# Four adjacency layers: another way to the bias of layer 0, denominators tile by tile, and a new order around the last tile

## The chip, the cores and the metric

The kernel runs on one core of one Trainium2 chip. The metric is device microseconds (us) of one execution. Engines: PE (TensorE, matmuls; PEld is its weight load), DVE (VectorE), ACT (ScalarE), POOL (GpSimd), SP (SyncE, which only issues DMAs here). ACT and POOL issue DMAs as well. Each engine works through its own instructions in order.

## The reference, cut to what matters

Four layers work on x of shape 8 x 2048 x 64 (batch B = 8, nodes N = 2048, channels C = 64) with one adjacency matrix; each is `x = layernorm(x + layer(x))`. The change lies in layer 0 and in what layer 0 prepares for layer 1:

```python
# layer 0: K = 3 terms x, A x, 2 A(A x) - x; weights and bias per node by an embedding of 16 numbers
w = einsum('nd,dkio->nkio', embedding, weight)
b = einsum('nd,do->no', embedding, bias)            # 2048 x 64
out = einsum('bnki,nkio->bno', x_g, w) + b
# layer 1, the part that layer 0's tiles prepare
h = x @ W
s = leaky_relu(h @ a_node, 0.2)
alpha = softmax(where(H.T > 0, s, NEG))             # 64 hyperedges over 2048 nodes
agg = einsum('ben,bnf->bef', alpha, h)
```

`agg` is a sum over nodes of exp(s) h for the members of each hyperedge, divided by a denominator, the sum of exp(s) over the same members.

## The kernel before, in words

Nodes go in 16 tiles of 128 (NT = 16), and a tile row holds all 8 batches, 512 columns (BC). Products with the mask of the adjacency matrix split their dense operand in a high and a low part, so each takes two matmuls. The stretch that matters has four parts.

**First product** (`first_product`, from L453): y1 = A x. Its 32 pieces of the matrix are numbered n = 0 to 31; `begin(n)` loads piece n (`raw`), makes the mask `m` from it on DVE (L519) and, for the first eight, loads x (`xraw`) and splits it on ACT (x_hi, L471) and DVE (x_lo, L472). `begin` runs two pieces ahead of the matmuls (L560), of which a piece has 16. PSUM buffers come in turn from one pool of seven (`ps_acc`): `warm`, four `y1p` per quarter, and two `bp`. Before the loop 16 warm-up matmuls run. At n = 1 `node_bias` (L476) makes the bias of all nodes: 16 matmuls of 16 rows by 64 columns from the transposed embedding `et`, loaded at the very start on ACT's queue (L1656). At n = 2 ACT copies them (`keep_bias`, L491) to `bn_all`. From n = 10 `midway` loads the weights of layer 0 and, last, the embedding `emb_sb` on SP's queue (L244). `steps` builds lists for layer 1 in between.

**Tiles of layer 0** (`layer0`, from L1075): the order is written out by hand in the loop from L1543, and `program_order` keeps PE, DVE, ACT and POOL to it. (SP's order is settled by the framework.) Each tile j has eight `weigh(j, g)`: 24 matmuls into one of two `pp` buffers (L1221), then four multiply-adds on DVE that read it (L1232). After each of them other steps are put: `normed(j - 1, 0..2)` normalises the tile before in three steps (sum, centring and square; variance and square root on ACT; reciprocal and scaling, and the store of x1 on SP's queue, L1259). After g = 4 comes `visit(j)`, the excursion: it gathers the weighted features of tile j - 2 into `aggp` (L1414), makes the second product of tile j + 1 (32 matmuls, L1184), masks for j + 2 on DVE (L449), comparisons of the matrix with its scaled mask on DVE (L1136), the transposes of x1 (`to_features`, L1309) and of y2 (`second_term`, L1194), and the degrees (L1203): one matmul with the mask's sum over POOL's `both` (L1131). After g = 5 and 7 `project` (L1364) multiplies with layer 1's weights (`hp`, L1336) and copies the results out (`hi` and `h` and `sc` on ACT, `lo` on DVE); `weights_of` (L1369) makes exp(s) in `es`, `weighted` (L1394) the weighted features on POOL. Transposes, degrees and `hp` share the two PSUM buffers `tr`.

**Last tile** (`last_tile`, L1497): tile 15 is normalised and projected in two halves of the batch (`half_normed`, `half_features`, `projected`, `copied`, `half_weighted`, `half_gather`). Before it `spread` (L1418) makes the membership masks `mds` of all 16 tiles anew, and `denominators` (L1429) multiplies them with `es`: 16 small fp32 matmuls, of two passes each, 15 of them in one run. `industry_early` (L1435) holds 16 steps of two matmuls of a product of layer 1 that needs nothing else; `early[0](n)` runs n of them wherever PE would wait.

**Start of layer 1** (`layer1`, from L584): `agg = aggp * rden` on DVE (L620), its exponential, transposes and two small products on PE (`fche` L645, `sep` L659, `dnp` L672), with `early` steps in between (L634, L641, L656); then the `ramp` (L1001), a hand-written order of the first units of work, in which `0.ind` runs what is left of `early`.

The order in the loop around g, which the change edits:

```python
                    elif g == 5:
                        ...
                        when(j - 1, project, 0)
                        if j == NT - 1:
                            half_normed(0, 0)
                            project(j - 1, 1)
                            weights_of(j - 1)
                    elif g == 6:
                        if j == NT - 1:
                            half_normed(0, 1)
                            weighted(j - 1)
```

## Time and profile before

| What | Value |
|---|---|
| Three runs | 1297.23, 1299.42, 1298.87 us; median 1298.87 |
| The profiled execution | 1296.06 us, its span 1294.3 us |
| PE busy, mean granted clock | 1228.0 us, 0.972 |
| First product | from 7.07 to 143.4 us (L560) |
| Weighing of layer 0's tiles | first L1221 at 157.13, last DVE step L1232 at 682.0 us |
| A whole tile in the middle | 32.66 us (from 628.26 to 660.92, the same matmul of two tiles) |
| `denp`, 32 matmul records L1431 | 7.0 us |
| `bp`, 32 matmul records L484 | 4.5 us |
| `agg` of layer 1, L620 | starts at 699.99 us |

How to read it: the profile is of one execution, and its times count from the start of the span. An fp32 matmul makes two records. "Idle before" is how long an engine did nothing before an instruction, with the instruction that released it. The granted clock is the share of full speed at which PE was allowed to run; a matmul at half clock counts as busy for twice as long. Pieces of the timeline name engine, line, operation, output and inputs.

### The profile page before, as it was taken

What the parts mean: (1) busy time and instruction counts of PE and PEld (TensorE: products, weight loads), DVE (VectorE), ACT (ScalarE), POOL (GpSimd) and SP (SyncE); (2) the same over time, 40 slices, a digit from 0 to 9 for tenths busy, and PEclk for the clock granted to TensorE, in tenths of its full rate; (3) what the DMA queues carried; (4) which work ended last, traced back from release to release, by engine and by line L of the source; (5) the groups of instructions that cost most, each with busy time, mean ns of one, the idle gap of its engine ahead of it and who ended that gap; (6) DMA issues with size and microseconds to landing.
All of it is one profiled execution on the core that took longest, in us unless ns stands there. A gap on an engine that the chain in (4) does not pass through costs nothing.

```text
span 1294.3 us, 19958 instructions
## 1 busy us (share of the span) xinstructions
PE 1228.0 (95%) x7598; PEld 1000.4 (77%) x7598; DVE 881.9 (68%) x1657; ACT 389.0 (30%) x987; POOL 503.4 (39%) x420
## 2 busy tenths in 40 slices
PE   9999989999999999999998799999998899999996
PEld 7877768888888888888886477777766788888885
DVE  5455378888787877777774777777774656565544
ACT  3000101222222222222232356666665521111111
POOL 1000282555555555555311678888871600000000
PEclk8999999999999999999997699999998999999998
DMA  8788742333333333332443222223220223324541
GB/s 293 195 237 207 187 122 89 103 108 104 105 107 102 105 106 106 105 108 96 168 134 98 89 91 101 99 92 105 83 69 1 98 99 129 128 101 155 192 173 68
DMA packets 100890, 157.23 MB, mean 121 GB/s; under 512 B 12785, under 2 KB 64113, under 8 KB 94897
## 3 DMA queue, kind: packets, MB, share of 16 engines
q1 hardware_dynamic: 98144, 151.51, 36.6%
q10 hardware_dynamic: 2464, 4.33, 0.9%
q8 instruction: 62, 1.02, 0.3%
q0 software_dynamic: 176, 0.02, 0.1%
q14 instruction: 44, 0.35, 0.1%
HBM read 118.08 MB, written 37.76 MB: 120 GB/s over the span
## 4 chain that ended last, share of the span: by engine, by line
PE 76%; DVE 9%; issue 7%; ACT 2%; DMA 2%; POOL 2%; SPq 0%; DVEq 0%; ACTq 0%; POOLq 0%
PE a L1671 18%; PE pp L1221 18%; PE ind L1671 9%; PE y2p L1184 9%; PE y1p L560 5%; DVE r L1232 5%; PE fc L914 3%; PE df L923 2%; PE gp L795 1%; PE yp L1771 1%; PE try L168 1%; PE trm L168 1%; PE hp L1336 1%; PE red L844 1%; DVE r L1241 1%
## 5 line engine op out<-in xcount | busy, mean ns | idle before, releaser
L1232 DVE SCALAR_TENSOR_TENSOR r<-pp,emb_sb,r 128x256 f32<-128x256 f32 x512 | 247.6, 484 | 87.9 <-PE pp L1221 72.5
L1221 PE MATMUL pp<-w_sb,xT 64*128 64x256 f32 x1024 | 160.3, 385 | 11.3 <-DVE r L1232 9.6
L1221 PE MATMUL pp<-w_sb,y2T 64*128 64x256 f32 x1024 | 156.7, 377 | 0.0
L1221 PE MATMUL pp<-w_sb,y1T 64*128 64x256 f32 x1024 | 156.7, 377 | 0.0
L1120 POOL TENSOR_TENSOR ms<-msk,srow 128x1024 f32<-128x1024 f32 x32 | 87.0, 2720 | 103.0 <-DVE msk L449 93.3
L1221 PEld LDWEIGHTS pp<-w_sb,xT 64*128 64x128 f32 x1024 | 97.8, 188 | 25.2 <-PE pp L1221 15.6
L1221 PEld LDWEIGHTS pp<-w_sb,y1T 64*128 64x128 f32 x1024 | 104.1, 188 | 8.2
L1221 PEld LDWEIGHTS pp<-w_sb,y2T 64*128 64x128 f32 x1024 | 103.9, 188 | 8.3
L560 PE MATMUL y1p<-x_hi,m 128*128 128x512 f32 x256 | 104.5, 408 | 0.7 <-ACT x_hi L471 0.7
L1184 PE MATMUL y2p<-y_hi,msk 128*128 128x512 f32 x256 | 102.5, 400 | 0.0
L560 PE MATMUL y1p<-x_lo,m 128*128 128x512 f32 x256 | 102.2, 399 | 0.2 <-DVE x_lo L472 0.2
L1671 PE MATMUL ind<-y_hi,mj_l 128*128 128x512 f32 x240 | 101.8, 424 | 0.2 <-DVE dlt L879 0.2
L1184 PE MATMUL y2p<-y_lo,msk 128*128 128x512 f32 x256 | 101.3, 396 | 0.0
L1671 PE MATMUL a<-v_hi,mj_l 128*128 128x512 f32 x256 | 100.1, 392 | 0.0
L1671 PE MATMUL a<-v_lo,mj_l 128*128 128x512 f32 x256 | 100.0, 391 | 0.0
L1671 PE MATMUL a<-y_lo,mj_l 128*128 128x512 f32 x240 | 95.1, 396 | 0.0
L1671 PE MATMUL a<-y_hi,mj_l 128*128 128x512 f32 x240 | 94.9, 395 | 0.0
L1671 PE MATMUL ind<-y_lo,mj_l 128*128 128x512 f32 x240 | 94.5, 394 | 0.0
L830 POOL TENSOR_TENSOR ez<-ez,coef 128x1024 f32<-128x1024 f32 x32 | 69.8, 2183 | 48.6 <-DVE ez L825 48.6
L1136 DVE SCALAR_TENSOR_TENSOR ms<-ms,adj 128x1024 f32<-128x1024 f32 x32 | 71.0, 2224 | 0.0
L1403 POOL TENSOR_TENSOR hs<-h,es 128x512 f32<-128x512 f32 x15 | 15.6, 1042 | 129.2 <-ACT hgr L1375 129.2
L560 PEld LDWEIGHTS y1p<-x_hi,m 128*128 128x128 f32 x256 | 49.1, 192 | 12.2 <-ACT x_hi L471 0.9
(298 smaller groups left out, 2410.5 us busy)
## 6 DMA issues: line engine op xcount, KB each, us to landing
mj_l<-mask SPq DMA_DIRECT2D x46, 1024.0 KB, 4.9
adj<-in_at SPq DMA_DIRECT2D x64, 256.0 KB, 3.9
mask<-msk SPq DMA_DIRECT2D x32, 512.0 KB, 4.0
raw<-in_at SPq DMA_DIRECT2D x31, 512.0 KB, 5.4
oh<-oh SPq DMA_DIRECT2D x32, 128.0 KB, 3.6
xT<-in_xt SPq DMA_DIRECT2D x16, 256.0 KB, 3.1
xs<-in_xn SPq DMA_DIRECT2D x16, 256.0 KB, 2.7
kept<-x SPq DMA_DIRECT2D x16, 256.0 KB, 2.0
```

The source lines that it names most:

```text
L168: nc.tensor.matmul(dst, src, ident, start=True, stop=True, is_transpose=True)
L560: nc.tensor.matmul(accs[q][jj], r_(m[:, t, jj * P:(jj + 1) * P]), r_(part[:, mt, :]), start=i + h + t == 0 and part is x_hi, stop=i == 3 a ...
L830: nc.gpsimd.tensor_tensor(by_b(ezs[i]), by_b(ezs[i]), per_b(t["coef"], 2 * i, 2), ALU.mult)
L914: nc.tensor.matmul(fc[:, h, :], fcw_sb[rs], sT[rs], start=True, stop=True)
L923: nc.tensor.matmul(df[:, b:b + 1], th[:, b % 2, (b // 2) * P:(b // 2 + 1) * P], av_sb, start=True, stop=True,)
L1120: nc.gpsimd.tensor_tensor(ms, m, srow[j].unsqueeze(1).to_broadcast([P, 8, P]), ALU.mult)
L1136: nc.vector.scalar_tensor_tensor(ms, ms, 1.0, raws[j][h], op0=ALU.mult, op1=ALU.not_equal, accum_out=bad[:, 2 * j + h:2 * j + h + 1],)
L1184: nc.tensor.matmul(acc, r_(msk[j, mt // 8][:, mt % 8, :]), r_(part[:, mt, :]), start=mt == 0 and part is y_hi, stop=mt == NT - 1 and part ...
L1221: nc.tensor.matmul(pp[:, h, pl, :], terms[j][name][rs, 2 * bq + pl], w_sb[rs, k, dq * 4 * C:(dq + 1) * 4 * C], start=k == 0, stop=k == K - 1,)
L1232: nc.vector.scalar_tensor_tensor(rb, ppv[:, :, dd, :], emb_sb[:, j, d:d + 1], rb, op0=ALU.mult, op1=ALU.add)
L1403: nc.gpsimd.tensor_tensor(b_view(hs), b_view(h_sb[:, j, :]), bcast(es[:, j, :]), ALU.mult)
L1671: nc.tensor.matmul(acc, r_(a[:, mt, :]), r_(part[:, mt, :]), start=mt == 0 and part is hi, stop=mt == NT - 1 and part is lo,)
```

## The change: what it does

The bias of layer 0 no longer comes from 16 thin matmuls. The embedding of eight tiles at a time (128 nodes by 8 x 16 numbers) is transposed on PE and copied by ACT, and one matmul per half multiplies it with `et[2]`, a block-diagonal matrix of eight copies of the bias, built by a memset and eight small loads on POOL's queue. For that the embedding is loaded before the loop on ACT's queue, and the transposed embedding and the separate bias are not loaded. The steps stand at n = 3 and n = 5, the copy out at n = 6. The warm-up matmuls alternate between two PSUM tiles.

`degrees` becomes `counted(j, i)`, which stands before `to_features` in the visit and adds the denominators of tile i = j - 3 of its argument, that is tile j - 2 of the visit: one fp32 matmul into the same PSUM tile and a second ACT copy; DVE adds it to `rden`. Only tiles 14 and 15 remain for `last_tile`. `spread` makes the mask of tile 15 alone.

The steps of `normed` move: 0 from after g = 0 to after g = 1, 1 from after g = 2 to the visit, 2 behind the first comparison of the visit (tile 14's stay). In the first tile the degrees, the second comparison and `scaled(1, 1)` move to after g = 2. In the last tile `project(14, 1)`, its weights and `industry_early` move, and `last_tile` has another order, with 6 + 3 + 1 `early` steps (before: 2); layer 1's start has 3 + 1 + 1 (before: 4 + 1 + 2), and `0.ind` runs the rest. `projected(15, 1)` takes a `pp` buffer instead of two `tr` ones. The cores of the diff:

```diff
-                nc.sync.dma_start(emb_sb, emb.rearrange("(t p) d -> p t d", p=P))
+                nc.scalar.dma_start(emb_sb, emb.rearrange("(t p) d -> p t d", p=P))
...
+                if step == 0:
+                    tr = ps_acc.tile([P, 2, P], F32, tag="acc", name="tr_et")
+                    for half in range(2):
+                        transpose(
+                            tr[:, half, :],
+                            emb_sb[:, half * NT // 2:(half + 1) * NT // 2, :]
+                            .rearrange("p t d -> p (t d)"),
+                        )
+                    for half in range(2):
+                        nc.scalar.copy(et[half][:, 0:P], tr[:, half, :])
+                    return
                 for half in range(2):
                     bp = ps_acc.tile([P, NT // 2, C], F32, tag="acc", name=f"bp_{half}")
...
+                    nc.tensor.matmul(
+                        bp.rearrange("p t c -> p (t c)"), et[half][:, 0:P], et[2],
+                        start=True, stop=True,
+                    )
...
+                for k in range(16):
+                    nc.tensor.matmul(warm[k % 2], ones, ones, start=True, stop=True)
                 begin(0)
                 begin(1)
+                midway(2 * K)
...
-                    if n == 1:
-                        node_bias()
-                    elif n == 2:
+                    if n in (3, 5):
+                        node_bias((n - 3) // 2)
+                    elif n == 6:
                         keep_bias()
...
-                early[0](4)
+                early[0](3)
...
-                early[0](2)
+                early[0](1)
...
+        def counted(j, i):
 
             dp = ps_tr.tile([P, QW], F32, tag="tr", name=f"dgp_{j}")
+            if j < NT:
+                nc.tensor.matmul(
+                    dp[:, 0:2], r_(msk[j, "sum"]), r_(ones_r), start=True, stop=True
+                )
+            if i >= 0:
+                nc.tensor.matmul(dp[:, 8:8 + B], mds[i], es[:, i, :], start=True, stop=True)
+                dens[i] = tile("den", f"den_{i}", (P, B), 1)
+                nc.scalar.copy(dens[i], dp[:, 8:8 + B])
+            if j < NT:
+                nc.scalar.copy(deg[:, j:j + 1], dp[:, 0:1])
...
             if j < NT - 1:
+                when(j - 1, normed, 1)
+            when(j + 1, compare, 0)
+            if j < NT - 1:
                 when(j - 1, normed, 2)
-            when(j + 1, compare, 0)
...
             when(j + 1, compare, 1)
+            counted(j + 1, j - 2)
             when(j - 1, to_features)
...
             when(j + 1, second_term)
-            when(j + 1, degrees)
+            if j == 2:
+                nc.vector.tensor_copy(rden, dens[j - 2])
+            elif j > 2:
+                nc.vector.tensor_tensor(rden, rden, dens[j - 2], ALU.add)
...
         def last_tile():
+            last = NT - 1
+            early[0](6)
             half_features(0)
+            gather(last - 1)
+            denp = ps_p.tile([P, 2, 2, 4 * C], F32, tag="pp", name="denp")[:, 0, 0, 0:B]
+            nc.tensor.matmul(denp, mds[last - 1], es[:, last - 1, :], start=True, stop=False)
+            projected(last, 0)
             half_normed(1, 0)
             half_normed(1, 1)
+            copied(last, 0, "sc")
+            weights_of(last, slice(0, 4))
+            copied(last, 0, "h")
+            copied(last, 0, "hi")
+            half_normed(1, 2)
             half_weighted(0)
+            copied(last, 0, "lo")
+            early[0](3)
+            half_features(1)
+            projected(last, 1)
+            copied(last, 1, "sc")
+            weights_of(last, slice(4, 8))
+            half_weighted(1)
+            early[0](1)
             half_gather(0)
+            nc.tensor.matmul(denp, mds[last], es[:, last, :], start=False, stop=True)
             half_gather(1)
+            nc.vector.tensor_tensor(rden, rden, denp, ALU.add)
...
+                        if j == NT - 1:
+                            normed(j - 1, 0)
                     elif g == 1:
+                        if j < NT - 1:
+                            when(j - 1, normed, 0)
+                        if j:
+                            when(j + 1, scaled, 1)
+                            when(j + 1, first_sum)
+                    elif g == 2 and j == NT - 1:
+                        normed(j - 1, 1)
+                    elif g == 2 and j == 0:
+                        compare(0, 1)
+                        counted(0, -1)
+                        scaled(1, 1)
...
                             half_normed(0, 0)
-                            project(j - 1, 1)
-                            weights_of(j - 1)
+                            early.extend(industry_early())
                     elif g == 6:
                         if j == NT - 1:
                             half_normed(0, 1)
+                            project(j - 1, 1)
+                            weights_of(j - 1)
                             weighted(j - 1)
...
+        et = [big.tile([P, BC], F32, tag=f"b1_{NT - 4 + q}", name=f"et_{q}") for q in range(3)]
+        nc.gpsimd.memset(et[2], 0.0)
+        for t in range(NT // 2):
+            nc.gpsimd.dma_start(et[2][t * D:(t + 1) * D, t * C:(t + 1) * C], bias0)
```

## The prediction, made before the changed kernel ran

> **What bounds the kernel now.** I read the page's shares first, then the PE clock in fine windows, then what PE waits for by stage, then the timelines at both ends of layer 0.
>
> ```profile
> PE 1228.0 (95%) x7598; PEld 1000.4 (77%) x7598; DVE 881.9 (68%) x1657; ACT 389.0 (30%) x987; POOL 503.4 (39%) x420
> PEclk8999999999999999999997699999998999999998
> ```
>
> PE is busy for 95% of the span and its clock is full except in three places of 32 us slices. So time can go only where PE idles, runs at half clock, or does work that is avoidable. The windows (columns: stretch, its length, busy time of PE, PEld, DVE, ACT, POOL, granted clock, DMA share, GB/s) show two such places:
>
> ```profile
> 11.00:15.00 4.00, 4.00 (x32) 3.64 (x31) 2.62 (x5) 1.22 (x3) 0.00 (x0) 0.92 1.00 359
> 15.00:19.00 4.00, 4.00 (x12) 3.21 (x12) 2.76 (x5) 1.14 (x2) 0.00 (x0) 0.50 0.93 315
> 19.00:23.00 4.00, 4.00 (x15) 3.18 (x14) 1.90 (x4) 2.11 (x4) 0.28 (x1) 0.73 0.88 332
> ...
> 680.00:684.00 4.00, 1.17 (x6) 0.49 (x3) 3.66 (x9) 0.79 (x2) 2.78 (x4) 0.92 0.20 66
> 684.00:688.00 4.00, 3.25 (x15) 2.30 (x15) 0.92 (x4) 1.34 (x8) 2.00 (x2) 0.50 0.00 0
> 688.00:692.00 4.00, 4.00 (x20) 4.00 (x20) 1.31 (x5) 0.51 (x3) 0.00 (x0) 0.50 0.18 68
> 692.00:696.00 4.00, 3.54 (x16) 2.85 (x17) 0.00 (x0) 0.37 (x1) 0.00 (x0) 0.50 0.00 0
> 696.00:700.00 4.00, 4.00 (x17) 3.20 (x14) 1.55 (x9) 1.33 (x8) 0.00 (x0) 0.50 0.00 0
> ```
>
> PE at half clock is "busy", but every other engine nearly stops in 688 to 696: PE alone is late there. The timeline names the work; the last column is the idle time before it.
>
> ```profile
> 11.44 4.48 PE L484 MATMUL bp<-bn_all,et 16*128 16x64 f32 x32
> 672.61 0.97 PE L1336 MATMUL hp<-wb,xT 64*128 64x130 f32 x7 [1.90 <-DVE y_lo L1362]
> 683.22 0.57 PE L168 MATMUL trx_last<-ident,x 128*128 128x128 f32 x2 [2.83 <-DVE x L1262]
> 686.93 5.29 PE L1431 MATMUL denp<-es,md 128*128 128x8 f32 x24
> ```
>
> In between, in layer 0's tiles (158 to 664 us), PE's waits are these (total, times, longest):
>
> ```profile
> PE pp L1221 <- DVE r L1232: 9.6, 16, 1.0
> PE try L168 <- ACT y L1190: 6.5, 15, 0.8
> PE dgp L1206 <- POOL both L1131: 3.0, 1, 3.0
> ```
>
> Two short waits a tile, and one of 3.0 us in the first tile.
>
> **What the Trainium skill says.** "TensorE: Matmul & The Clock Gate", Part 1: PE's clock has two states, half after a window of about 3.4 us with too little activity, full after a busy one. The trace agrees: the granted clock is 0.50 or 1.00 in whole spells, and they begin after the thin bias matmuls and after the waits of 1.90 and 2.83 us; waits of 0.4 to 0.7 us never cause one. "DMA: Bandwidth & Descriptors", SWDGE vs HWDGE vs iDMA: queues of different issuers share the 16 DMA engines, which take turns between them. The trace of before has no long ACT load beside SP's, so this only bounds a cost below. "ScalarE: Activation LUTs", What ACT_TABLE_LOAD costs: about 1283 ns; the trace has 1283 ns at L1251. The moved sqrt keeps one load per tile, so nothing is added.
>
> **The change, part by part** (minus is a gain; "W n" is piece n of the first product).
>
> *Bias.* Removed: 32 records of L484 hold PE from 11.44 to 15.85, 4.4 us. After them 12 y1p matmuls run 0.427 us apart instead of 0.229: 2.4 us. PE is the late one there (from 15.85 to 44 it never waits, and DVE's masks wait for PE 4.2 us). Added: two transposes, about 0.25 (four take 0.5 at L168), and two fp32 matmuls of 512 columns, four passes of 0.23: 1.2 in all. Net -5.6. Against it: PSUM turns otherwise. The pool has 7 buffers; two warm tiles and tr_et shift the order so that y1p_4 takes y1p_0's buffer and must wait for y_lo (42.87 to 44.3), and each next one for a 0.69 us y_lo where PE needs 0.46: +0.8. And the embedding: it now leaves ACT's queue behind the second x_hi cast, at 11.1. In 4.9 us (its landing in before) it is there at 16, before PE reaches W 3 at about 18.4. If instead its 128 rows of 64 B per DMA engine (2048 over 16) alternate with SP's 2 KB rows, at 359 GB/s or 0.091 us a row, it takes 12 us and lands at 25: PE idles 6.6 us, falls to half clock for a window (+1.6), and the part ends at +3.4. I take +0.8, since 18.4 leaves 2.4 us of slack. The warm-up in two tiles: 0; its records are 0.164 us apart with 0.19 of LDWEIGHTS each, so the shared tile isn't what paces them; should it end at 4.6 instead of 6.36, a half-clock window from about 8 costs 1.6, half of it behind the wait for W 2's data. The four et loads leave the first megabyte of traffic: at most -0.3. Sum -4.0, bounds -6 to +3.4. The eight small loads and the memset on POOL (1.0 us each at L528) lie in POOL's wait of 21.4 us before 22.7; without that cover they would cost 9 us of POOL. ACT's issue of 0.43 lies in its idle 2.2 us at 11.1. The later stretch to 143 us passes the gain on: PE's waits there are on list steps that PE itself paces.
>
> *First tile.* dgp moves from after the second to after the third weigh; `both` ends at 165.50, PE arrives at 165.0 rather than 162.4: wait 0.4 instead of 3.0, -2.6. compare(0, 1) goes to the same place, in DVE's slack of 1.5 us. scaled(1, 1) stays in POOL's busy chain.
>
> *Denominators per tile.* Two passes more a tile, 0.25 us (16 such records take 1.95 at L659), and dgp's 0.2 come before the transposes of x, where PE waits 0.40 for y2. So they are covered, and dgp's 0.2 after try2 is gone. But `tr` has two buffers: try2 now takes dgp's, and waits for two ACT copies behind y (0.16 each, overlapping, plus signal): about +0.25. Net +0.05 a tile, +0.8 over 15; bounds -0.2 to +0.3 a tile, -3 to +4.5. Behind the waiting try2 stand PE's pp matmuls, and nothing else. DVE's added 0.17 (rden) sits in its 2.2 us wait before the sixth weigh.
>
> *Norm steps.* Step 0 one weigh later: DVE does 1.95 a weigh against PE's 2.6, plus 1.5 for the step. Before, the fourth weigh's buffer was late by 0.7. Now the second STT cannot start before its own weigh has ended, so the fifth is late by the same 0.7: nothing gained. Step 1 (0.68) joins the visit, where DVE keeps 2.2 - 0.85 us of slack; ACT's y1T copy waits for its sqrt, 15 us before use. The store of x1 leaves SP 1.9 us later, for a reader 400 us away. Nothing: 0.
>
> *Last tile.* Moving project(14, 1) behind the seventh weigh removes the 1.90 wait and the half-clock window that follows (two weighs in 7.2 us instead of 5.2 + 0.6). By DVE's chain x is then ready at 679.3 and the transposes go at 679.4 instead of 683.22; six industry steps (12 x 0.229 = 2.75) fill the wait from 676.3. After that the chain is: hs_lo 680.6, hp 681.5, pow 682.3, x 682.9, xT 684.05, hp 684.6, weights 685.65, hs 686.2, last gather 686.6, rden 686.8, y_lo 687.3. `agg` starts there instead of 699.99: -12.7. Of this 6.6 us is the 30 denominator records at half clock, the rest idle and half clock. PE's work in 683 to 690 is thin, so a half-clock window lands there; what runs in it is industry filler before `he` is ready, and dnp: +0.7. Sum -12.0, bounds -13.5 to -7.
>
> *Layer 1's start.* Its fillers shrink (3, 1, 1); they lay in waits for ACT. The remainder in the ramp shrinks from 7 steps (717.97 to 721.2) to one. ACT's ST copy of unit 1 then waits for t3 (ends 719.98), so gates start at 720.3 instead of 722.42: -2.1. With a chance that the clock stays at half longer without them: -1.7, bounds -2.7 to 0.
>
> Sum: -4.0 - 2.6 + 0.8 - 12.0 - 1.7 = -19.5. The profiled execution took 1296.06 (span 1294.3 and 1.8 around it): 1276.6. The median of the runs is 2.8 above it, 1298.87, so 1279.4.
>
> **Rivals.** (1) The embedding lands late: the alternation above; for it is that 128 rows a DMA engine is many turns, against it that the load of before landed in 4.9 us beside a busy SP queue. Start +3.4 instead of -4.0: 1286.8. (2) The end keeps less: half clock holds through layer 1's head and stretches fche, sep and the ramp. For it: PE has only 1.6 us of work in the 3.4 us from 683.6. Then -7 in place of -13.7: 1286.1. (3) The 0.7 us gap per tile does vanish, if DVE stands further ahead than I think: 15 x 0.7 more, 1268.9. (4) Slower: the wait before try2. If den's copy comes late enough that 0.4 becomes 1.9, the size that brought half clock at 672.6, each visit loses 1.5 and 3.4 us at half clock, 1.7: 3.2 a tile, 45 over 14, ending at 1324. It decides from 6 tiles on (19.5 / 3.2). Against it: the copies are 0.16 us and their matmuls end before y does. (5) 1, 2 and the upper bound of the tiles together: -19.5 + 7.4 + 6.7 + 3.7, 1297.2: no change.
>
> **How the numbers follow.** Forecast 0.58, (1) 0.15, (2) 0.12, (3) 0.05, (4) 0.06, (5) 0.04. From 1272 to 1290 holds the forecast with the bounds of its parts not all at one end, and (1) and (2); it leaves out (3), (4), (5), 0.15. Faster by over 0.2% (2.6 us, about what a measurement can tell from no change): 0.90; within: 0.04; slower: 0.06.
>
> **What would show it.** No half-clock stretch between 15 and 21 us, and the first y_hi evacuation near 39 instead of 42.87; if PE waits for the embedding over 2 us before tr_et, rival 1. One `dgp` wait under 0.6. A tile period within 0.3 of 32.66 us (660.92 - 628.26, the two pp gaps). No wait of hp on y_lo, trx_last about 3.8 us sooner after the last weigh but one, and `agg` 12 to 13 us sooner counted from the last tile's start. I am wrong if the tile period moves by over 0.5 us, or if the span between the last weigh and `agg` stays above 14 us.

## The result, and the profile after

The changed kernel takes 1277.61 us, median of four runs (1276.43 to 1278.5), beside 1299.14 for the kernel before (four runs, 1297.23 to 1300.43): a ratio of 0.9835, 95% interval 0.9818 to 0.9852. The forecast was 1279.4 with a range of 1272 to 1290. The profiled execution took 1278.5 (span 1276.8); that of before took 1296.06 (span 1294.3) and was 3 us below its median. So the spans differ by 17.5 and the medians by 21.5 us. Marks and stretches below are read from the traces, each of one execution; totals are medians.

The page of the changed kernel, its shares and its granted clock:

```profile
PE 1218.1 (95%) x7572; PEld 986.7 (77%) x7572; DVE 889.9 (70%) x1672; ACT 387.1 (30%) x1003; POOL 506.0 (40%) x426
PEclk9999999999999999999998799999998999999998
```

PE is still busy for 95%, with 10 us less of busy time. The windows (stretch, length, PE, PEld, DVE, ACT, POOL, granted clock, DMA share, GB/s) show what became of the two half-clock places of before:

```profile
11.00:15.00 4.00, 4.00 (x18) 3.11 (x17) 3.36 (x6) 1.35 (x3) 0.00 (x0) 1.00 1.15 283
15.00:19.00 4.00, 4.00 (x20) 3.26 (x19) 1.86 (x4) 1.14 (x2) 0.00 (x0) 1.00 1.04 399
19.00:23.00 4.00, 4.00 (x19) 3.29 (x18) 2.12 (x5) 1.24 (x3) 1.32 (x4) 1.00 0.87 307
...
672.00:676.00 4.00, 4.00 (x23) 2.83 (x19) 3.79 (x13) 1.48 (x5) 2.78 (x4) 1.00 0.25 66
676.00:680.00 4.00, 3.21 (x20) 2.25 (x19) 2.45 (x7) 1.83 (x10) 1.81 (x2) 1.00 0.01 2
680.00:684.00 4.00, 3.54 (x23) 2.69 (x22) 2.65 (x16) 1.78 (x10) 0.14 (x2) 1.00 0.38 131
```

The clock is 1.00 in all of them, at the start and at the end of layer 0, where `agg` begins at 684.10 instead of 699.99. What PE waits for between 140 and 690 us (total, times, longest):

```profile
PE pp L1236 <- DVE r L1247: 6.6, 16, 0.9
PE try L168 <- ACT deg L1224: 4.8, 15, 0.8
PE pp L1236 <- issue: 3.9, 1, 3.9
PE dgp L1216 <- POOL both L1140: 2.5, 1, 2.5
```

The waits of `hp` and `trx_last` are gone. Two things are not as forecast: the wait for `both` still stands with 2.5 us, and there is a single wait of 3.9 us that the profile puts down to "issue".

To see where the gain lies I cut the span at three marks: the first tile's `dgp`; **T2**, the first transposes of y1 for tile 2 (`try`, in the excursion of tile 1); and `agg`. Differences are after minus before.

| Stretch | Before | After | Difference | Forecast |
|---|---|---|---|---|
| start to first `dgp` | 165.55 | 161.11 | -4.4 | -4.0 |
| `dgp` to T2 (first tile and a half) | 41.61 | 44.20 | +2.6 | -2.6 |
| T2 to `agg` (tiles and last tile) | 492.83 | 478.79 | -14.0 | -11.2 |
| `agg` to the end | 594.31 | 592.70 | -1.6 | -1.7 |
| span | 1294.3 | 1276.8 | -17.5 | -19.5 |

The sum came out because two errors of opposite sign nearly cancel: the first tile lost 2.6 instead of gaining it, and the tiles gained more than I gave them. That they cancel is luck.

**The 3.9 us.** Timelines of DVE and POOL in the first tile, behind the sixth weigh, where four small products and reductions make layer 1's score weights (`score_weights`, L1651), and PE's wait behind them. First the kernel before:

```profile
187.70 1.27 POOL L1124 TENSOR_TENSOR cs<-msk 128x512 f32<-128x512 f32 x1
188.53 0.52 DVE L1629 TENSOR_TENSOR prod<-wb,vecs 64x64 f32<-64x64 f32 x1
...
190.67 0.25 DVE L1629 TENSOR_TENSOR prod<-wb,vecs 64x64 f32<-64x64 f32 x1
...
193.35 0.70 PE L1221 MATMUL pp<-w_sb,xT 64*128 64x256 f32 x4 [1.65 <-issue]
```

And the changed kernel:

```profile
181.13 2.35 POOL L1129 TENSOR_TENSOR ms<-msk,srow 128x1024 f32<-128x1024 f32 x1
181.49 2.07 DVE L1651 TENSOR_TENSOR prod<-wb,vecs 64x64 f32<-64x64 f32 x1
183.45 1.26 POOL L1133 TENSOR_TENSOR cs<-msk 128x512 f32<-128x512 f32 x1
183.84 0.94 DVE L1651 TENSOR_TENSOR prod<-wb,vecs 64x64 f32<-64x64 f32 x1
184.78 0.72 POOL L1134 TENSOR_TENSOR cs<-cs 128x256 f32<-128x256 f32 x1
185.04 0.54 DVE L1651 TENSOR_TENSOR prod<-wb,vecs 64x64 f32<-64x64 f32 x1
...
188.55 1.23 PE L1236 MATMUL pp<-w_sb,xT 64*128 64x256 f32 x4 [3.89 <-issue]
```

The same product takes between 0.25 and 2.07 us. Each of the four, the shortest too, ends within 0.1 us after the POOL instruction that was running when it started (183.56 and 183.49; 184.78 and 184.71; 185.59 and 185.51; 186.12 and 186.04). It is so in all 14 profiles of this study, for 56 products of 0.24 to 2.39 us. The Trainium skill, "SBUF — State Buffer", Who interferes with whom, fits this: a DVE instruction with two inputs in SBUF takes the second through a read port that GpSimd shares, and the shared pair is an exclusive lock. Both inputs of these products lie in SBUF; the weighing steps read one operand from PSUM and keep their 0.5 us. The longest product met the long one on POOL (`ms`, 2.35 us), which in the kernel before had ended by then. So the block of eight took 4.9 us instead of 2.6, and PE stood 3.89 instead of 1.65. In all nine profiles with these steps behind the sixth weigh, PE's wait there is the sum of the four products and 0.07 to 0.09 us more (1.57 and 1.65 before, 3.81 and 3.89 after). Then the clock was at half from 187.9 to 194.7 (the last matmul line: 1.23 us instead of 0.70). PE worked in it from 188.55 on, which lost about another 3.1.

### The profile page after: what moved, and what is told of

Its sections match the earlier page's. It is cut to its first block, busy times and chain, and to the rows that moved or that the text cites. A ratio compares the mean times of both kernels' runs of the same rounds, so it can differ in the third digit from the quotient of the medians.

```text
span 1276.8 us, 19960 instructions
## 1 busy us (share of the span) xinstructions
PE 1218.1 (95%) x7572; PEld 986.7 (77%) x7572; DVE 889.9 (70%) x1672; ACT 387.1 (30%) x1003; POOL 506.0 (40%) x426
## 4 chain that ended last, share of the span: by engine, by line
PE 72%; DVE 9%; issue 3%; ACT 3%; POOL 2%; DMA 1%; SPq 0%; ACTq 0%; DVEq 0%; POOLq 0%
PE pp L1236 19%; PE a L1694 18%; PE ind L1694 9%; PE y2p L1193 9%; DVE r L1247 5%; PE fc L923 3%; PE df L932 2%; PE gp L804 1%; PE yp L1793 1%; PE try L168 1%; PE trm L168 1%; PE red L853 1%; PE dp L822 1%; PE hp L1357 1%; DVE r L1256 1%
## 5 line engine op out<-in xcount | busy, mean ns | idle before, releaser
L1236 PE MATMUL pp<-w_sb,xT 64*128 64x256 f32 x1024 | 159.2, 386 | 10.5 <-DVE r L1247 6.6
L1129 POOL TENSOR_TENSOR ms<-msk,srow 128x1024 f32<-128x1024 f32 x32 | 81.0, 2532 | 110.2 <-DVE msk L449 98.7
L1133 POOL TENSOR_TENSOR cs<-msk 128x512 f32<-128x512 f32 x32 | 62.7, 1961 | 0.0
```

Source lines behind the costliest of these rows:

```text
L1129: nc.gpsimd.tensor_tensor(ms, m, srow[j].unsqueeze(1).to_broadcast([P, 8, P]), ALU.mult)
L1133: nc.gpsimd.tensor_tensor(cs, m[:, 0:4], m[:, 4:8], ALU.add)
L1236: nc.tensor.matmul(pp[:, h, pl, :], terms[j][name][rs, 2 * bq + pl], w_sb[rs, k, dq * 4 * C:(dq + 1) * 4 * C], start=k == 0, stop=k == K - 1,)
```

## The experiments

Each edit is made to the changed kernel unless said otherwise. Ratios are to the kernel before, measured beside each. Medians of the kernel before lay between 1293.9 and 1299.1 from group to group, so across groups only ratios and stretches of the trace are compared. The changed kernel again, the measure for these:

> The changed kernel again, as the measure for the three beside it. Both theories: 0.9835 of the kernel before, within 0.2%; 1275.5 to 1278.

1278.53 us, ratio 0.9848 (0.9825 to 0.9872). Its stretches: `dgp` 161.82, then 42.66, 478.75, 593.87. Against the kernel before that is -3.7, +1.1, -14.1 and -0.4 where the table has -4.4, +2.6, -14.0 and -1.6. So only T2 to `agg` repeats within 0.1 us; `dgp` to T2 moves with the length of the half-clock spell behind the 3.9 us wait (here 3.4 us instead of 6.8), and the stretch after `agg` with the spells there.

**1. The first tile undone.**

```diff
                         if j == 0:
                             compare(0, 0)
+                            compare(0, 1)
                             load_weights()
...
+                        if j == 0:
+                            counted(0, -1)
-                        if j:
-                            when(j + 1, scaled, 1)
-                            when(j + 1, first_sum)
+                        when(j + 1, scaled, 1)
+                        when(j + 1, first_sum)
...
-                    elif g == 2 and j == 0:
-                        compare(0, 1)
-                        counted(0, -1)
-                        scaled(1, 1)
```

> The changed kernel with the first tile's part undone: the second comparison after the first weigh, degrees and scaled(1, 1) after the second. The prediction put this part at -2.6 us, so by it this kernel takes 2.6 us longer than the changed one: 1280.2. Theory from the trace: the part is worth nothing, because the wait for `both` only moved (2.97 before, 2.51 after) and the loss behind it, at the score weights after the sixth weigh, depends on how POOL and DVE meet. PE now reaches the first tile 6.6 us sooner while POOL's start is held by a load, so the dgp wait should be 5 to 6 us, with a half-clock spell behind it, and the wait at the score weights should be near the 1.65 of before, without a spell of its own. Sum: +3.5 and +1.7 to +3.4 at dgp, -2.2 and -3.4 at the score weights: 1277 to 1279.

1277.45 us, ratio 0.9847 (0.983 to 0.9864): no difference from the changed kernel. Waits of PE in it:

```profile
159.72 0.37 PE L1216 MATMUL dgp<-ones_r,both 128*128 128x2 f32 x1 [5.27 <-POOL both L1140]
...
190.56 0.70 PE L1236 MATMUL pp<-w_sb,xT 64*128 64x256 f32 x4 [1.53 <-issue]
```

The wait for `both` is 5.27 with a half-clock spell from 159.2 to 166.0, and the wait at the score weights is back at 1.53, without one. So the part gains at its own place (a weigh more is done ahead of `dgp`) and gives it back three weighs later. The theory holds in both numbers; its claim that the part is worth nothing too. The prediction's 2.6 is at the edge of the interval, and the two waits speak against it.

**2. The score weights in the excursion**, ahead of the y2 transposes, where DVE waits for PE.

```diff
             when(j - 1, to_features)
+            if j == 0:
+                score_weights()
...
                     elif g == 5:
-                        if j == 0:
-                            score_weights()
```

> The changed kernel with one step moved: the four small products and reductions that make layer 1's score weights stand in the first tile's excursion, before the y2 transposes, where DVE waits 2.1 us for PE and 2.1 us more afterwards, instead of behind the sixth weigh. Theory: in the changed kernel these steps held DVE for 4.9 us behind the sixth weigh, PE stood 3.89 us and then ran 6.8 us at half clock (3.4 lost); both go, 7.3 us less, 1270.3. Rival one: the half-clock spell there has another cause, or comes anyway at the wait for both of 2.5 us; then only the wait goes, 3.9 us less, 1273.7. Rival two: the steps merely move the stall to the y2 transposes or to the first weigh after the excursion; no change, 1277.6.

1271.49 us, ratio 0.9796 (0.9778 to 0.9813), about 5 to 7 us below the changed kernel. From `dgp` to T2 it takes 37.29 instead of 42.66 to 44.20: the wait and its spell are gone, 5.4 to 6.9 us. The products are as slow as in the changed kernel (2.39, 0.95, 0.55, 0.25 us), but PE does not wait for them. By the trace the stall, and not the clock alone, was the cause; rivals one and two fall. The expected total of 1270.3 was missed by 1.2: in the profiled run a spell of 6.8 us stood at the first transposes instead.

**3. The norm steps in their old places.**

```diff
+                        when(j - 1, normed, 0)
                     elif g == 1:
-                        if j < NT - 1:
-                            when(j - 1, normed, 0)
...
-                    elif g == 2 and j == NT - 1:
-                        normed(j - 1, 1)
+                    elif g == 2 and j:
+                        when(j - 1, normed, 1)
...
-                when(j - 1, normed, 1)
+                when(j - 1, normed, 2)
             when(j + 1, compare, 0)
-            if j < NT - 1:
-                when(j - 1, normed, 2)
```

> The changed kernel with the norm steps of tiles 1 to 14 back in their old places (0 after the first weigh, 1 after the third, 2 ahead of the excursion's first comparison). The prediction gave this part 0: the gap only goes from one weigh to the next; by it 1277.6. Theory from the trace: the wait per tile fell from 0.56 to 0.33 because step 0's second half no longer meets a POOL instruction (0.85 to 0.69 us), so this kernel's tile period is near 32.7 instead of 32.47 and it takes 13 x 0.23 = 3.0 us longer: 1280.6.

1277.64 us, ratio 0.9854 (0.9834 to 0.9873). The medians can't tell it from the changed kernel. The trace can: the wait per tile is 0.56 again, the period 32.69 (591.91 to 624.60) instead of 32.47 (594.54 to 627.01), and T2 to `agg` takes 481.63, 2.8 more. The wait in two neighbouring tiles, here and in the changed kernel:

```profile
591.91 0.70 PE L1236 MATMUL pp<-w_sb,xT 64*128 64x256 f32 x4 [0.56 <-DVE r L1247]
...
624.60 0.70 PE L1236 MATMUL pp<-w_sb,xT 64*128 64x256 f32 x4 [0.56 <-DVE r L1247]
```

```profile
594.54 0.70 PE L1236 MATMUL pp<-w_sb,xT 64*128 64x256 f32 x4 [0.33 <-DVE r L1247]
...
627.01 0.70 PE L1236 MATMUL pp<-w_sb,xT 64*128 64x256 f32 x4 [0.33 <-DVE r L1247]
```

The theory's 3.0 holds in the trace. In the total it is hidden by what varies: in this profile the first `dgp` came at 159.72, 1.4 to 2.1 us sooner than in the two profiles of the changed kernel, and the stretch after `agg` was 0.9 to 2.1 shorter.

**4. The old order of the last tile**, with the denominators still made tile by tile: `last_tile` in its old sequence with the old numbers of `early` steps, and `project(14, 1)` after the sixth weigh.

```diff
                             half_normed(0, 0)
-                            early.extend(industry_early())
+                            project(j - 1, 1)
+                            weights_of(j - 1)
```

> The changed kernel with the last tile's old order (second projection of tile 14 after the sixth weigh, no early steps ahead of the halves, two before the last sum, and 4 and 2 in layer 1's start), but with the denominators still made tile by tile. It shows how the 12.2 us that the last tile gained divide. The prediction: 6.6 us are the 30 denominator records at half clock, the rest idle and half clock that the order removes, so here 5.6 us are lost: 1283.2, with a wait of hp near 1.9 and of trx_last near 2.8 and the half clock from there. Rival one: the denominators lay beside a chain on DVE, ACT and POOL that is as long without them, so the order made nearly all of it: 1288 or more. Rival two: the denominators made nearly all of it: 1279 or less.

1285.12 us, ratio 0.9911 (0.9895 to 0.9928). T2 to `agg` takes 484.71, 5.9 more than the 478.79; the prediction's split gave 5.6. The waits of `hp` and `trx_last` are back, with half clock from 677.0 to 687.2:

```profile
666.87 0.80 PE L1357 MATMUL hp<-wb,xT 64*128 64x130 f32 x7 [1.90 <-DVE y_lo L1383]
...
675.79 0.41 PE L168 MATMUL trx_last<-ident,x 128*128 128x128 f32 x2 [2.84 <-DVE x L1277]
```

A further 2 to 3 us lie after `agg` (595.86 against 592.70 to 593.87): the old order leaves more early steps for layer 1's ramp, which is the prediction's last term; this was not tried alone.

**5. The denominators in one run again**, in the new order.

```diff
-            nc.tensor.matmul(denp, mds[last - 1], es[:, last - 1, :], start=True, stop=False)
+            for t in range(last):
+                nc.tensor.matmul(denp, mds[t], es[:, t, :], start=t == 0, stop=False)
...
-            counted(j + 1, j - 2)
+            when(j + 1, counted, -1)
```

> The changed kernel with its new last tile, but the denominators of tiles 0 to 14 in one run of 30 matmul records there (all masks made anew by POOL at the end), as before. It takes the tile-by-tile denominators alone out of the change. By difference (14.0 us from the first y1 transposes of tile 2 to agg, less 2.8 for the norm steps and 5.9 for the order) they are worth 5.3 us: 1283.8 beside the changed kernel's 1278.5; the prediction had 6.6 for the records at half clock less 0.8 for the tiles, 5.8. Rival one: in the new order the run finds idle time of PE to lie in, and at full clock takes 15 x 0.25 = 3.7 us: 2 us or less are lost, 1280.5. Rival two: the masks on POOL come ahead of the last tile's weighted features and hold them up: 8 us or more, 1287.

1278.51 us, ratio 0.9879 (0.9862 to 0.9895), 4 to 6 us above the changed kernel by the ratios; T2 to `agg` 481.79, 3.0 more. The run:

```profile
674.10 3.52 PE L1521 MATMUL denp<-es,md 128*128 128x8 f32 x30
```

Thirty records take 3.52 us here; before, 24 of them took 5.29. So the expected 5.3 was too high for this part alone, and rival one named the right length of the run but not that PE has little idle time for it. Up to the last weighing step this kernel is 1.3 us faster, which is what making them tile by tile costs (0.1 us a tile); behind it, 4.3 slower. The 4.3 are more than the run. Right behind it the clock falls to half, from 677.3 to 680.7 (columns as in the windows above):

```profile
674.00:677.00 3.00, 3.00 (x28) 2.96 (x27) 0.59 (x2) 0.42 (x1) 1.02 (x1) 1.00 0.00 0
677.00:681.00 4.00, 4.00 (x19) 3.31 (x19) 1.29 (x7) 1.19 (x8) 0.00 (x0) 0.57 0.08 32
```

PE is busy all through, and had waited 0.69 us at most in the 10 us before. The eleven profiles with the new last tile and without the run have no half clock between the last weighing step and `agg`. So a run of thin matmuls was followed by half clock with PE busy, as with the bias before (from 11.44, half clock from 14.3).

Of the 14.0 us, the norm steps are 2.8, the order 5.9, the denominators 3.0 net, and 2.3 are left, which belong to order and denominators together: in the old order the run itself stood in half clock, in the new one only what follows it. That this is all of the 2.3 is not shown.

**6. The start of before.**

```diff
-                    if n in (3, 5):
-                        node_bias((n - 3) // 2)
-                    elif n == 6:
+                    if n == 1:
+                        node_bias()
+                    elif n == 2:
                         keep_bias()
```

> The changed kernel with the start of before: the transposed embedding and 16 thin bias matmuls at the second piece, one warm-up tile, the embedding last on SP's queue. The prediction: 4.0 us more. Theory from the trace: in the first tile PE waits for POOL's `both` (2.5 us in the changed kernel), and POOL's chain starts when the row of scales has been loaded, which follows the first product's end; so what the bias gains arrives there whole: `both` ended 4.4 us sooner than before, and this kernel loses 4.4 us up to that matmul and in all. Rival: the chain's start hangs on SP's queue and not on the first product, so only part of it arrives: 2 us or less.

1279.73 us, ratio 0.985 (0.9823 to 0.9877) beside 0.9848: unclear. In the trace the first y_hi comes at 43.18 instead of 37.97 to 38.34, and `dgp` at 164.51 instead of 161.11 to 161.82. The kernels with the new start in which PE waits for `both` have that `dgp` between 159.5 and 161.8, so the start is worth 2.7 to 5.0 us up to there, and it did not show in the total.

**7. Tile 0's sums first.** With the score weights moved, POOL adds the mask's halves ahead of the products that need the row of scales.

```diff
+            summed(0, 0)
+            summed(0, 1)
             scaled(0, 0)
             scaled(0, 1)
```

> The kernel with the score weights in the excursion, and one thing more: for tile 0 POOL adds up the mask's halves and `both` ahead of the two products with the row of scales, in the 11 us in which it waits for that row, instead of after each of them. Theory: the dgp wait of the first tile (1.8 to 2.5 us where no half clock stands before it) is POOL's chain alone, 5.3 us of which is taken out of it; the wait goes and none takes its place, since POOL stays 5 us ahead: up to 2.5 us below the kernel with the score weights moved, 1269 to 1271.5. Rival one: POOL's next tile or DVE's comparison becomes the late one in the first excursion, and nothing is gained: 1271.5. Rival two: the sums collide with DVE's last evacuations of the first product (two SBUF inputs each) and delay the first transposes by 1 to 2 us: 1272 to 1273.

1269.67 us, ratio 0.979 (0.9767 to 0.9813), 8.9 below the changed kernel beside it. `both` ends at 146.43 instead of 161, PE no longer waits for it, and `dgp` comes at 158.08. The first tile's wait was POOL's chain, held by a load. Most of the 8.9 is experiment 2, whose ratio was 0.9796: what this step adds in the total is within the intervals.

**8. Norm step 0 in two pieces**, the sum after the second weigh and the centring after the third.

```diff
                     elif g == 1:
                         if j < NT - 1:
-                            when(j - 1, normed, 0)
+                            when(j - 1, normed, -1)
...
+                    elif g == 2 and j:
+                        normed(j - 1, 0)
```

> The changed kernel with norm step 0 cut in two: the sum over channels after the second weigh, the centring and the square after the third, instead of both after the second. Theory: DVE has 0.55 us to spare in each weigh (2.59 against 2.04) and a second pp buffer gives the same again, so a step of up to 1.1 us makes PE wait for nothing and one of 1.37 us for 0.3; two pieces of 0.7 wait for nothing. The wait of 0.33 a tile goes: tile period 32.14, 13 x 0.33 = 4.3 us less, 1273.3. Rival one: the two pieces together are still 1.37 us over two weighs with 1.1 to spare, so the same 0.3 is paid in two parts: no change, 1277.6. Rival two: the later square makes the variance late in the excursion: up to 1 us a tile more, 1280 to 1290.

1266.51 us, ratio 0.9768 (0.9746 to 0.979), 12 us below the changed kernel beside it: more than the theory. First the same transposes of two neighbouring tiles in this kernel, whose distance is the period; then the wait that went, as it stood in the changed kernel:

```profile
596.45 0.66 PE L168 MATMUL try<-ident,y 128*128 128x128 f32 x4 [0.23 <-ACT deg L1224]
...
628.32 0.66 PE L168 MATMUL try<-ident,y 128*128 128x128 f32 x4 [0.23 <-ACT deg L1224]
```

```profile
593.62 0.60 PE L1236 MATMUL pp<-w_sb,y2T 64*128 64x256 f32 x4
594.54 0.70 PE L1236 MATMUL pp<-w_sb,xT 64*128 64x256 f32 x4 [0.33 <-DVE r L1247]
595.05 0.63 PE L1236 MATMUL pp<-w_sb,y1T 64*128 64x256 f32 x4
```

The period is 31.87, so 0.60 less and not 0.33. The second piece shows why: such groups of four matmuls follow each other by 0.43 us elsewhere, but across the wait it is 0.92, and 0.51 after it. The idle time is counted from the end of the matmul before, which in a full pipeline overlaps the next one. T2 to `agg` is 8.5 us shorter. By the spans the whole is 13.5: another 1.6 lie before T2, where tile 0's step was cut too, and 3.4 after `agg`, where this kernel has 34.5 us of half clock and the one beside it 47.2.

**9. The three together (2, 7 and 8).**

> The changed kernel with the three moves that gained alone put together: the score weights in the excursion, tile 0's sums ahead of its products with the row of scales, norm step 0 in two pieces. Theory: they act at different places, so they add: 8.9 us of the first two and 12.0 of the third off the 1278.5 of the changed kernel beside them, of which 3 us of the last were half-clock spells in layer 1's ramp that fell differently: 1258 to 1261. Rival: the first tile and the steady tiles share DVE's slack (the score weights and the split step meet in the first tiles), and half of the smaller gain is lost: 1262 or more.

1261.41 us, ratio 0.9743 (0.9723 to 0.9762). They add in the trace: 36.66 from `dgp` to T2 (37.24 in experiment 7), 470.26 from there to `agg` (470.23 in experiment 8). The total is just above the expected 1258 to 1261.

**10. One ACT copy** of degree and denominator, on top of these. (The edit also lets the square root of the norm step write over its input.)

```diff
-                nc.scalar.copy(dens[i], dp[:, 8:8 + B])
+            lo, hi = 2 * (j == NT), 2 + B * (i >= 0)
+            kept_d = tile("den", f"den_{j}", (P, 2 + B), 1)
+            nc.scalar.copy(kept_d[:, lo:hi], dp[:, lo:hi])
+            dens[i] = kept_d[:, 2:2 + B]
             if j < NT:
-                nc.scalar.copy(deg[:, j:j + 1], dp[:, 0:1])
+                nc.scalar.copy(deg[:, j:j + 1], kept_d[:, 0:1])
```

> The three moves together, and the degree and the denominator of the excursion copied out of PSUM by one ACT copy of 10 columns instead of two copies; the degree is copied on from there. It sizes the wait for the shared PSUM buffer. Theory: the y2 transposes wait 0.23 us a tile for the second of two ACT copies of 0.16 that stand behind the y2 activation; one copy takes 0.16 off that: tile period 31.7 instead of 31.87, 14 x 0.16 = 2.2 us off. Rival one: the wait then falls to the end of the y2 activation itself, 0.1 us earlier: 1 us or less. Rival two: the buffer is not what the transposes wait for: no change in the period.

1258.46 us, ratio 0.9724 (0.9702 to 0.9745). The wait of the y2 transposes falls from 0.23 to 0.17 and the period from 31.87 to 31.80 in most tiles, and in two tiles, where the wait had been 0.71 and 0.51, by over 0.3. T2 to `agg` is 1.5 us shorter (468.77 against 470.26), between rival one's 1 and the theory's 2.2. The two copies had overlapped. This kernel has the lowest median of all, but its interval overlaps that of experiment 9. It is 1.1 to 1.3% below the changed kernel by the ratios and 2.76% (2.55 to 2.98) below the kernel before.

**11. The start of before on kernel 10.**

> The kernel with all four moves, and the start of before (16 thin bias matmuls at the second piece). Theory: the start's gain is 4.8 us where the first y_hi is made, and 4.0 of it reached the first tile's dgp in the changed kernel, where PE waits for POOL; the half-clock spells after the waits of the first tile, which come in some runs and not in others, then covered it in the medians (1279.7 against 1278.5). Without those waits it arrives whole: 4.8 us more than the kernel beside it with the new start. Rival one: the start's gain is taken up by the load of the row of scales whatever follows: 2 us or less. Rival two: the prediction's 4.0.

1262.25 us, ratio 0.9749 (0.9729 to 0.9769): 3.8 us more. The trace has the first y_hi at 41.60 against 37.75 and `agg` at 668.55 against 664.54, 4.0 later. With the waits of the first tile out of the way, the start's gain arrives whole, as the theory had it. Its size is the prediction's 4.0 (rival two of this run) and not 4.8, but that may be chance: in the old start the half-clock spell was 3.4 us long here and 6.8 in the kernel before and in experiment 6, which fits that the first y_hi differs by 3.9 here and by 4.8 to 4.9 there.

## Why the prediction was right, and where it was wrong

The total was right, but its closeness is in part luck: two terms were wrong in opposite directions, and half-clock spells move single stretches by up to 3.4 us between profiles of the same work.

**Bias and start: right.** Forecast -4.0; -4.4 at `dgp` (-3.7 in the repeat), and 3.8 to 4.0 in experiment 11. In experiment 6 it was there in the trace and not in the total. No half clock between 15 and 21 us, and the first y_hi at 37.97 where I wrote "near 39". The embedding landed 5.1 us after its issue, at 15.2, and its transposes started at 18.69 without a wait: rival 1 is out. The 0.8 that I booked against it, for the slack of 2.4, was not needed, nor was the 0.8 for the PSUM buffers: PE has no wait over 0.1 us between 37 and 45, where it would show.

**First tile: wrong.** The step that failed is "wait 0.4 instead of 3.0, -2.6". `both` ended 4.4 us sooner, but PE came sooner too, so 2.51 of the wait stayed, in spite of a weigh more ahead of it. The working had taken PE's arrival from the profile of before, and there a half-clock spell that I had not seen, from 147.5 to 150.9 behind a wait of 2.16 us at the first transposes, made PE late by up to 1.7. The profile of after has the same wait and no spell. In the kernels with the new start and this first tile the wait at `dgp` goes with that spell: 1.80 to 2.51 us without one, 0.51 and 0.10 with one of 3.4 us (experiments 4 and 5), none with one of 6.8 (2 and 8):

```profile
161.11 0.27 PE L1216 MATMUL dgp<-ones_r,both 128*128 128x2 f32 x1 [2.51 <-POOL both L1140]
...
159.52 0.27 PE L1216 MATMUL dgp<-ones_r,both 128*128 128x2 f32 x1 [0.51 <-POOL both L1140]
```

(The changed kernel, then experiment 4.) So the 0.4 was right for a run with that spell. The -2.6 was not: the weigh more ahead of `dgp` is a real gain (experiment 2 takes 37.29 us from `dgp` to T2 instead of 41.61, the 1.65 of the score weights and 2.7), but it was lost behind the sixth weigh, at the score weights: 2.24 us more of waiting and 3.1 of half clock. The wait of 1.65 there was in the profile of before, under "issue", and I left it out of the list of PE's waits in the tiles. It also looked harmless, since it brought no half clock. What I had not asked is which POOL instruction DVE's products would meet once the order around them shifted. Experiments 1 and 2 show it from both sides.

**Denominators per tile: right.** Forecast +0.8; 1.3 by experiment 5. The wait on the shared PSUM buffer is real (the transposes now wait for ACT's `deg`, 0.23 each), and it has the size given, not the size of rival 4.

**Norm steps: wrong, by a little.** The step "nothing gained: 0" failed. The tile period stayed within the 0.3 us that I allowed, and the gap did move to the next weigh, but it shrank from 0.56 to 0.33, 2.8 us over the tiles (experiment 3). The centring, which reads two operands from SBUF, takes 0.69 instead of 0.85 in its new place; that it met POOL in the old one fits the timelines but was not tested alone. Rival 3 asked whether the whole gap could go. It can, by the cut of experiment 8. Its price of 0.7 a tile was nearly right: 0.22 from the new places (32.69 to 32.47) and 0.60 from the cut, 0.82.

**Last tile: right.** Forecast for all from T2 to `agg` -11.2; it is -14.0, and without the norm steps' 2.8 it is -11.2. Experiments 4 and 5 divide it as above. I wrote that 6.6 us were denominator records at half clock; more exactly, 3.5 of these are the records at full clock, and the rest is the half clock in which they stood. The old order's waits bring that spell without the run too, but it lasts 10.2 us then (experiment 4) and not 17.1. The predicted marks are there: no wait of `hp` on y_lo; counted from the last y2 transposes of layer 0 (642.99 before, 639.27 after), `agg` 12.2 us sooner and `trx_last` 4.0; 9.1 us between the last weighing step and `agg` instead of 17.5, below the limit of 14. The +0.7 for a spell between 683 and 690 did not come: the clock stays full until 693.0 (687.2 in the repeat).

**Layer 1's start: right.** Forecast -1.7, measured -1.6. It is the weakest figure, since this stretch varies from 590.5 to 593.9 between kernels that do not differ in it, and the repeat has -0.4. A mark inside it is firmer. The gates of unit 1 start 22.4 us after `agg` before, and 20.4 to 20.6 in ten of the twelve profiles with the new start of layer 1 (19.3 and 22.8 in the others). The working had 20.3 (720.3 with `agg` at 699.99).

Rival 2 (half clock eats the end's gain) is out by the windows above, and rival 5 with its parts. In the 45 us after `agg` the changed kernel still spends 27.3 us at half clock, the kernel before 24.3.

How much idling brings half clock was the weak point of the whole working. "TensorE: Matmul & The Clock Gate", Part 1, gives a window of about 3.4 us and a rule against idle gaps longer than that. I had read waits of 1.90 and 2.83 as enough, and the traces agree that shorter ones can be. In these profiles no single wait up to 1.65 us in layer 0 was followed by a spell, and all seven of 3.5 to 5.3 were. In between it went either way: 2.16 us at the first transposes in 8 of 14 profiles, 1.90 at `hp` once and once not, 2.77 yes, 2.83 and 2.84 at `trx_last` yes, 1.80 to 2.97 at `dgp` no. What decides there stays open. In layer 0's tiles a spell cost at most 1.7 or 3.4 us, half its length, and two profiles with the same work there can differ by that much.

## What to carry to other kernels

When a step is moved so that one engine runs ahead of another, list every later place where the two meet: a small DVE instruction with both operands in SBUF cost here what was left of the POOL instruction it met, and a wait that was harmless at 1.65 us cost 1.4 to 1.8 times its length at 3.9, because it brought half clock with it. A gain made before such a meeting point counts only if the meeting point moves with it. Cut a step that is longer than an engine's spare time per beat into pieces that each fit, before looking for a better place for the whole.

## What was not expected of the hardware

- PE's idle time in the profile understates a wait in a running pipeline: 0.33 us shown was worth 0.60.
- A run of thin matmuls was followed by half clock though PE was busy: 30 `denp` records from 674.10, half clock from 677.3 (experiment 5); 32 bias records, half clock 2.9 to 3.5 us after their start in all three profiles that have them, and none there in the other eleven.
- 128 KB in rows of 64 B, issued by ACT at 10.08 us beside SP's 512 KB loads, landed in 5.1 us (5.1 to 6.1 in eleven profiles), about as quickly as a load of 512 KB on SP's queue (5.3).
- The eight small loads on POOL's queue were issued in 4.28 us, 0.5 each and not the 1.0 that the page of before had led me to.
